# A two-layer block on one core: a joined gate, earlier statistics, lent tiles for the fifth scan, and a reordered end

## The chip, the core and the metric

The kernel runs on one core of one Trainium2 chip. The metric is the device time of one execution in microseconds (us), here always of that core. The engines are TensorE (PE in the profile, its weight loads PEld), VectorE (DVE), ScalarE (ACT), GpSimd (POOL) and SyncE (SP), which issues most DMAs. Each engine works through its own queue in the order in which the program wrote its instructions, and waits on semaphores for the others.

## The reference, cut to what matters

The input x has 4 batches of 256 tokens of width 512, in float32. Layer 0 adds an attention with small latents and a gated FFN of width 1792, both on the normalized x. Layer 1 adds a selective state-space model (below) and a top-2 mixture of LoRA experts over a dense product, again on the normalized x.

```python
proj = hidden_states @ in_proj_w            # 512 -> 2 * 1024
x, z = jnp.split(proj, 2, axis=-1)
xc = silu(conv4(x))                         # causal taps along time, per channel
ssm_p = jnp.einsum('bdl,ed->ble', xc, x_proj_w)
dt_r, Bm, Cm = rmsnorm of ssm_p[:32], [32:48], [48:64]
dt = softplus(dt_r @ dt_proj_w.T + dt_bias)
def step(h, inp):                           # over 256 time steps, 1024 channels x 16 states
    dA = jnp.exp(dt_t[..., None] * A)
    h = dA * h + dt_t[..., None] * B_t[:, None, :] * x_t[..., None]
    return h, jnp.einsum('bdn,bn->bd', h, C_t)
y = (ys + D_param[None, :, None] * xc) * silu(z)
out = jnp.einsum('bdl,hd->blh', y, out_proj_w)
```

## The kernel before, in words

The program is written out by hand in one function, and a schedule by hand fixes the order of each engine's queue. Layer 0 takes up the first 285 us: layer norm, attention of batches 0 to 3, and beside it the FFN as a generator `ff` whose pieces `go(ff, n)` puts between the attention's steps. `gate_up` makes the hidden values, `down` multiplies them by the down projection and adds the result to x. For token blocks 5, 6 and 7 the sum is kept in PSUM, and `add_last` adds it later, within layer 1.

Layer 1 works on one batch after another. The scan of a batch is cut into 32 units: 8 chunks c of 128 channels, times 4 groups g of 4 states each. `NU` is 4, `PER` is 32, and the loop at L1370 has one pass u for each of the 128 units, and two more. A unit consists of:

- `decays(u)`, ACT: four exponentials of dt times A into a tile of 128 x 1024 (L978). The loop issues it two units ahead.
- `scan_in(u)`, DVE: bx, the product of the B row and the spread dt*x (L984).
- `scan(u)`, DVE: the scan itself into a tile h (L999), and on POOL the product hc of h and the C row (L1004).
- `states_sum(u)`, PE: adds hc over the states into ysum in PSUM (L1016). For the first group of a chunk it begins ysum with D times xc (L1014). It is issued in pass u + 1.

When the four groups of a chunk are summed, `take_sum` copies ysum out (L1021, on ACT; on DVE for the very first), two units after the last group's scan. One unit later `gate` multiplies it by silu(z) on POOL (L1024). `ysum` has one buffer, so the next chunk's sum begins after `take_sum`.

Between these, `put(b, s, f, ...)` places other work at unit s of batch b, ahead of that unit's bx; `put_mid` places it between bx and scan, `put_late` behind the scan. In batch b this other work is: the rest of dt for the same batch (`step_in` on PE and ACT into tile `u`, `step_exp` on ACT into `u`, `lw` and `e`, `step_out` and `step_x` on POOL); dt and dt*x sent to DRAM and read back with each channel spread over the partitions of its states (`send`, L931, and `spread`, L937, both on SP); z's projection (`pz_mm`, L946) and its silu (`gate_silu`, L952, with a table load before and after it); and for the next batch b + 1 the norm (`norm_stats`, `norm_scale`, `norm_turn`, `norm_copy`), x's projection (`px_mm`, L755), the convolution (`conv_in`, `conv_taps`, `conv_out`; some taps as matmuls, L802, some on POOL, L809), its silu (`conv_silu`, L818), the product with x_proj (`pp_mm`, L829) and its rms norm (`pp_square`, `pp_norm`, L843). Batch 0 also loads the late weights (`load_late`, L1232: rl for the router, lb, bw, ow), and batches 0 and 2 hold the `router` and the choice of experts (`route`). The output of batch b - 1 is multiplied in batch b (`out_mm`, L1112). For the last batch it follows in a list `late` at the end of the loop, from unit 118 on; then `out_x` copies each half to x (L1117) and issues its store (L1118).

A tile of a pool with a tag shares the buffers of that tag: a new tile waits until all who use the old one in that buffer are done, also where they stand later in the program. Four cases matter here. The PSUM tag `mm` has 3 buffers. The weight tag `w_in` has 3, and `weights` issues its load on SP (L621), so a load whose buffer is not free holds SP's whole queue. The tags `u`, `e` and `lw` have one each. The pool `act`, with tiles h (2), hc (3), sz (3) and two of the three decay tiles, is opened at the end of pass 2 in the memory of the FFN's hidden values (`open_act`), and so can be written only after the last down projection. This is why the first scans take their tiles from others: `lent` names, for units 0 to 3, the tags in which decays, h and hc lie.

Of the kernel before, what the change touches and what calls it, by code (L numbers as in the profile page):

```python
# [8 lines left out]
F32 = mybir.dt.float32  # L9
# [3 lines left out]
ALU = mybir.AluOpType  # L13
# [28 lines left out]
def block_kernel(  # L42
# [508 lines left out]
    ff = gate_up(0)  # L551
    masks()

    def maxima(b, pieces, second, side=()):

        side = dict(side)
        for k in range(8):
            for hp in range(2):
                scores_max(b, k, hp)
            for f, *args in side.get(k, ()):  # L560
                f(*args)
            go(ff, pieces[k])
            if k in (3, 5, 7):
                put_max(b, k // 2 - 1)
            go(second, 1)
        go(second)
# [41 lines left out]
    ff = gate_up(1)  # L608
    attention(2, ff, True, 6)
    norm = normalize(2)  # L610
    attention(3, ff, False, 5, {k: [(next, norm)] for k in range(6)})
    go(ff, 1)
    weigh(3, 7)
    att.close()
# [97 lines left out]


    def norm_stats(b):
        mv = w1.tile([P, 2, 2], F32, tag="mv1", name="mv1", bufs=2)
        for i in range(2):
            st = w1.tile([P, 6], F32, tag="st1", name="st1", bufs=2)
            nc.vector.bn_stats(st, x[:, 2 * b + i, :])
            nc.vector.bn_aggr(mv[:, i, :], st)
        rs = w1.tile([P, 2], F32, tag="rsn", name="rsn", bufs=2)  # L720
        inv_root(rs, mv[:, :, 1], eps[:, 0:1])
        live["ln", b] = mv, rs
# [226 lines left out]
    def gate_silu(b, *ps):  # L949
# [5 lines left out]


    lent = {
        "d": ("d", "w_in", "d", "w_in"), "h": ("w_in", "u", "e", "u"),
        "hc": ("w_in", "lw", "w_in", "lw"),
    }  # L960

    def lend(n, u):
# [149 lines left out]
        mm(live["po", b, i], lhsT=xcs[b][:, c, i * P : (i + 1) * P], rhs=late_w["ow"][:, c, :],  # L1112
           start=False, stop=(c == DC - 1))

    def out_x(b, i):
        tb = 2 * b + i
        nc.scalar.copy(x[:, tb, :], live.pop(("po", b, i)))  # L1117
        nc.sync.dma_start(out_d[tb * P : (tb + 1) * P, :], x[:, tb, :])  # L1118


    def load_x(b, p):
# [128 lines left out]
    for b in range(B):  # L1250
# [14 lines left out]
        else:  # L1265
# [5 lines left out]
            put_late(b, 2, step_x, b, 1)  # L1271
            put(b, 4, load_z, b, 1)
            put(b, 9, load_late, "rl")
            put(b, 11, load_late, "lb")
            for k in range(4):
                put(b, 14 + 2 * k, load_late, "bw", k, 4)
            for k in range(DC):
                put(b, 21 + k, load_late, "ow", k, DC)
            for p, u in ((0, 3), (1, 8)):
                for i in range(2):  # L1280
                    put(b, u, pz_mm, b, p, i)
            put(b, 4, gate_silu, b, 0)
            put(b, 12, gate_silu, b, 1)
            put_late(b, 1, add_last, 5)
            put_late(b, 3, add_last, 6)
            put_late(b, 4, add_last, 7)
# [14 lines left out]
            put(b, 3 if c == 2 and not b else 4 * c - 6 + o, spread, "dt", b, c)  # L1301
            put(b, 4 * c - 4 + o, spread, "du", b, c)
        put(b, 10, load_z, b, 2)
        put(b, 12, load_z, b, 3)
        for p, at_i, at_g in ((2, (14, 15), 16), (3, (22, 24), 25)):
            for i in range(2):
                put(b, at_i[i], pz_mm, b, p, i)
            if p == 3 or nxt == B:
                put(b, at_g, gate_silu, b, p)
        if nxt < B:  # L1310
# [11 lines left out]
                put(b, 8 + o + 2 * p, conv_in, nxt, p)  # L1322
                put(b, 9 + o + 2 * p, conv_taps, nxt, p)
            put(b, 16 + o, conv_out, nxt, NP - 1)
            put(b, 16 + o, conv_silu, nxt, (b, 2))
            put(b, 17 + o, pp_mm, nxt, 0)
            put(b, 18, pp_mm, nxt, 1)
            put(b, 19, pp_square, nxt)
# [19 lines left out]
            for k, u in enumerate((27, 28, 29, 31)):  # L1348
                put(b, u, pz_mm, nxt, k // 2, k % 2)
            if b % 2 == 0:  # L1350
                for i, u in enumerate((16, 19, 20, 21)):
                    put(b, u, router, b, i)
                put(b, 25, route, b)
            put(b, 26, expert_turn, b)
# [11 lines left out]
            put(b, 21, expert_out, b, 1)  # L1366

    total = B * PER
    late = []
    for u in range(total + 2):  # L1370

        last = u - 2
        shut = (last // PER, last % PER // NU) if last >= 0 and last % NU == NU - 1 else None
        if shut and shut != (0, 0) and u < total:
            take_sum(*shut)
        if 3 <= u < total - 2:
            decays(u + 2)
        for f, a in at.get(u, ()):
            f(*a)
        if u < total:  # L1380
            if u:
                scan_in(u)
            for f, a in mid_at.get(u, ()):
                f(*a)
        if shut == (0, 0):
            take_sum(0, 0)
        if u > total:
            b, c = shut
            nc.vector.tensor_tensor(xcs[b][:, c, :], ysum, szs[b, c // 2][:, c % 2, :], ALU.mult)
        if u < total:  # L1390
            scan(u, 1 if u < total - 1 else 4)
            if u < 3:
                decays(u + 2)
        if u < total and u > NU + 1 and u % NU == 2:
            gates = (u - NU - 2) // NU
            gate(gates // DC, gates % DC)
        for f, a in late_at.get(u, ()):
            f(*a)
        if late and u >= total - PER + 22:
            c = late.pop(0)  # L1400
            for i in range(2):
                out_mm(B - 1, i, c)
        if total > u > total - PER and u % NU == 2 and (u - NU - 2) // NU >= total // NU - DC:
            late.append((u - NU - 2) // NU % DC)
        if u > total:
            late.append(DC - 1)
        if 1 <= u <= total:
            states_sum(u - 1)
        if u < 3:
            go(ff, (9, 12, 100)[u])  # L1410
        if u == 2:
            open_act()
    for i in range(2):
        for c in late:
            out_mm(B - 1, i, c)
        out_x(B - 1, i)


# [99 lines left out]
```

## Time and profile before

| what | us |
|---|---|
| median of 4 runs (lowest to highest) | 842.02 (839.02 to 843.23) |
| the profiled execution, its own time | 841.21 |
| its span, first to last instruction | 839.4 |
| start of scan 0, of scan 32 (batch 1), of scan 127 | 326.19, 467.34, 825.39 |
| last matmul of the down projection ends | 346.9 |
| last copy of the output ends | 836.1 |
| busy: PE, DVE, ACT, POOL | 749.6, 654.1, 552.8, 497.0 |
| granted TensorE clock, mean | 0.953 |

A line of a timeline gives the start, the duration of a group of like instructions in a row, the engine, the line of the kernel, the operation, the tile written and the tiles read, the shape, and the count. A bracket gives the idle time of that engine before it and who ended the wait. Matmuls in float32 appear as two records each, so "x8" is four matmuls. Lines of the page's second part hold one digit per fortieth of the span (21 us): the busy share in tenths.

### The profile page before, as it was taken

The numbers are of one execution on the slowest core, as the hardware profiler recorded it, in microseconds if no ns is written. First come the engines' busy times: TensorE is split into PE (matmuls) and PEld (weight loads), VectorE is DVE, ScalarE is ACT, GpSimd is POOL, SyncE is SP. The second block draws the span as 40 slices with busy tenths as digits, with TensorE's granted clock in tenths as the row PEclk, the third lists the DMA queues.
The fourth block names the chain that finished last, engine by engine and source line by source line (L and its number), as shares of the span: only waits on it lengthen the run. The fifth ranks groups of instructions, "written<-read, shape, count | busy, mean of one in ns | idle before, by whom it ended". The sixth has DMA issues, their size and how long they took to land.

```text
span 839.4 us, 11100 instructions
## 1 busy us (share of the span) xinstructions
PE 749.6 (89%) x3846; PEld 430.4 (51%) x3846; DVE 654.1 (78%) x602; ACT 552.8 (66%) x1113; POOL 497.0 (59%) x389
## 2 busy tenths in 40 slices
PE   5999999999999999999787899997999987957874
PEld 3665546566555667666443457444357544313321
DVE  4587755387734446796899999999999999999994
ACT  4335575335556377689796898886998886856460
POOL 3233321002333424687869799779799679798763
PEclk9999999999999999979899999989999989997997
DMA  7234322002233322457663554444552435253200
GB/s 225 76 89 127 100 76 63 0 1 55 70 86 82 108 39 79 135 139 186 146 158 102 150 154 125 111 113 126 157 158 88 113 94 143 65 155 109 83 18 25
DMA packets 68642, 86.71 MB, mean 103 GB/s; under 512 B 12221, under 2 KB 52169, under 8 KB 68458
## 3 DMA queue, kind: packets, MB, share of 16 engines
q1 hardware_dynamic: 58938, 66.08, 29.2%
q0 software_dynamic: 9072, 18.35, 7.8%
q10 hardware_dynamic: 576, 1.57, 0.5%
q8 instruction: 30, 0.49, 0.2%
q14 instruction: 26, 0.21, 0.1%
HBM read 66.58 MB, written 10.22 MB: 91 GB/s over the span
## 4 chain that ended last, share of the span: by engine, by line
PE 47%; DVE 28%; ACT 12%; POOL 7%; issue 4%; DMA 2%; SPq 0%; DVEq 0%; ACTq 0%; POOLq 0%
DVE h L999 17%; PE pg L444 6%; ACT decay L978 6%; PE pu L444 5%; PE po L469 5%; DVE bx L984 5%; POOL hc L1004 5%; PE px L755 4%; PE av L397 4%; PE ysum L1016 2%; PE scT L386 2%; PE px L802 2%; DVE mpl L354 2%; PE po L1112 2%; PE po L464 2%
## 5 line engine op out<-in xcount | busy, mean ns | idle before, releaser
L1004 POOL TENSOR_TENSOR hc<-h,cr 128x1024 f32<-128x1024 f32 (+1 forms) x130 | 301.9, 2324 | 75.7 <-DVE h L999 59.7
L999 DVE TENSOR_TENSOR_SCAN h<-decay,bx 128x1024 f32<-128x1024 f32 (+1 forms) x129 | 288.2, 2236 | 26.1 <-POOL hc L1004 4.9
L978 ACT ACTIVATE decay<-dts,aneg 128x255 f32<-128x255 f32 x504 | 213.3, 501 | 52.7 <-DVE h L999 42.6
L984 DVE TENSOR_TENSOR bx<-brow,dus 128x1024 f32<-128x1024 f32 x128 | 157.7, 1232 | 7.1 <-DMA dus<-dud 2.8
L1016 PE MATMUL ysum<-hc,stack 128*32 128x256 f32 x1024 | 87.3, 417 | 39.6 <-POOL hc L1004 39.5
L456 POOL TENSOR_TENSOR hlo<-g,hhi 128x512 fp32r<-128x512 f32 x28 | 35.8, 1280 | 117.3 <-ACT hhi L455 117.3
L354 DVE TENSOR_REDUCE mpl<-sc 128x4 f32<-128x1024 f32 x64 | 76.7, 1219 | 23.6 <-PE sc L352 22.1
L427 POOL DMA_DIRECT2D wgu<-in_wgu x56 | 31.0, 555 | 90.8 <-PE pg L444 89.6
L1112 PE MATMUL po<-ow,xc 128*128 128x512 f32 x128 | 70.9, 659 | 12.0 <-POOL xc L1024 11.4
L388 ACT ACTIVATE pe<-scT 128x1024 f32<-128x1024 f32 x64 | 64.0, 1023 | 22.9 <-PE sc L352 14.3
L1016 PEld LDWEIGHTS ysum<-hc,stack 128*32 128x32 f32 x1024 | 21.1, 111 | 99.1 <-POOL hc L1004 63.2
L946 PE MATMUL pz<-xn1T,w_in 128*128 128x256 f32 x256 | 71.4, 429 | 0.0
L755 PE MATMUL px<-xn1T,w_in 128*128 128x256 f32 x256 | 62.7, 392 | 0.4 <-ACT sz L952 0.3
L946 PEld LDWEIGHTS pz<-xn1T,w_in 128*128 128x128 f32 x256 | 51.8, 212 | 20.9 <-issue 13.4
L755 PEld LDWEIGHTS px<-xn1T,w_in 128*128 128x128 f32 x256 | 48.7, 194 | 13.8 <-issue 3.4
L452 DVE SCALAR_TENSOR_TENSOR g<-g,pg 128x512 f32<-128x512 f32 x28 | 19.2, 686 | 45.5 <-ACT g L451 45.5
L469 PE MATMUL po<-wd,hhi 128*128 128x512 f32 x112 | 49.2, 439 | 0.0
L444 PE MATMUL pg<-xhi,wgu 128*128 128x512 f32 x112 | 48.8, 435 | 0.0
L444 PE MATMUL pu<-xhi,wgu 128*128 128x512 f32 x112 | 47.7, 426 | 0.8 <-DVE g L454 0.8
L455 ACT CAST hhi<-g 128x512 fp32r<-128x512 f32 x28 | 17.3, 619 | 45.8 <-DVE g L454 45.8
L444 PE MATMUL pu<-xlo,wgu 128*128 128x512 f32 x112 | 44.5, 397 | 0.0
L444 PE MATMUL pg<-xlo,wgu 128*128 128x512 f32 x112 | 44.1, 394 | 0.0
(236 smaller groups left out, 1271.4 us busy)
## 6 DMA issues: line engine op xcount, KB each, us to landing
dts<-dtd SPq DMA_DIRECT2D x124, 128.0 KB, 2.8
dus<-dud SPq DMA_DIRECT2D x124, 128.0 KB, 3.1
wgu<-in_wgu POOLq DMA_DIRECT2D x56, 256.0 KB, 2.7
w_in<-in_inz SPq DMA_DIRECT2D x16, 512.0 KB, 4.7
w_in<-in_inx SPq DMA_DIRECT2D x14, 512.0 KB, 4.3
dtd<-dt SPq DMA_DIRECT2D x15, 256.0 KB, 2.2
dud<-du SPq DMA_DIRECT2D x15, 256.0 KB, 2.2
wd<-in_wd POOLq DMA_DIRECT2D x7, 512.0 KB, 3.5
```

What stands on the lines that cost most here:

```text
L354: nc.vector.tensor_reduce(mpl2[b % 2][:, qb, 2 * hp : 2 * hp + 2, 16 + 2 * gq : 18 + 2 * gq], sc.rearrange("p i (f k) -> p i f k", f=2), A ...
L388: nc.scalar.activation(pes[b, k][:, 2 * t : 2 * t + 2, :], sc, AF.Exp)
L444: mm(ps, lhsT=wgus[i][:, hc, :], rhs=xs[j][:, hc, :], start=(hc == 0 and j == 0), stop=(hc == HC - 1 and j == 1))
L469: mm(po, lhsT=hids[th][j][:, m, i * P : (i + 1) * P], rhs=wd[:, m, :], start=False, stop=(m == MC - 1 and j == 1))
L755: mm(px[:, i, :], lhsT=w[:, i, hc, :], rhs=xns[b][:, hc, :], start=(hc == 0), stop=(hc == HC - 1))
L946: mm(pz[:, i, :], lhsT=w[:, i, hc, :], rhs=xns[b][:, hc, :], start=(hc == 0), stop=(hc == HC - 1))
L978: nc.scalar.activation(da[:, k, 1:], live["dts", b, c][:, k, 1:], AF.Exp, scale=aneg[:, c, k, g : g + 1])
L984: nc.vector.tensor_tensor(bx, brow[g // 2][:, g % 2, :].unsqueeze(1).to_broadcast([P, NG, S]), live["dus", b, c], ALU.mult)
L999: nc.vector.tensor_tensor_scan(h[:, n].rearrange("p n t -> p (n t)"), da[:, n].rearrange("p n t -> p (n t)"), bx[:, n].rearrange("p n t -> ...
L1004: (nc.vector if k == NG - 1 else nc.gpsimd).tensor_tensor(hc[:, n], h[:, n], crows[b][:, g, :].unsqueeze(1).to_broadcast([P, NG // parts, ...
L1016: mm(ysum[k * NB : (k + 1) * NB, :], lhsT=stack, rhs=hc[:, k, :], start=False, stop=(g == NU - 1))
L1112: mm(live["po", b, i], lhsT=xcs[b][:, c, i * P : (i + 1) * P], rhs=late_w["ow"][:, c, :], start=False, stop=(c == DC - 1))
```

## The change

- The statistics (bn_stats, bn_aggr) of batch 1's norm move from unit 2 of batch 0 into layer 0, at step 6 of the last attention; a function `moments` holds them, with one buffer per tag.
- The fifth scan (unit 4) takes h from tag `e` and hc from tag `u`, no longer from `act`.
- The copy of the very first sum, on DVE, stands behind the scan of unit 5, not ahead of it.
- In batch 0 the projection of z's pair 1 moves from unit 8 to units 11 and 12, its silu from unit 12 to the convolution's silu at unit 17, and the gate of chunk 2 to that of chunk 3 at unit 18. Pair 2's projection moves from units 14 and 15 to 15 and 16, the first `router` from 16 to 18.
- In batch 0 the load of z's pair 3 moves from unit 12 to 17, lb from 11 to 22, bw from 14, 16, 18, 20 to 18 to 21, ow from 21 to 28 to 22 to 29.
- In the last batch each gate stands one unit earlier, in the pass of its `take_sum`; the sum over states stands ahead of the output matmuls of the list `late`.
- The last gate, on DVE, is cut into two halves of 128 tokens. The second half of the output is copied by DVE and stored from ACT's queue.

```diff
@@ -550,6 +550,13 @@
     hidden(0)
     ff = gate_up(0)
     masks()
+
+    def moments(b, pool):
+        mv = live["mv"] = pool.tile([P, 2, 2], F32, tag="mv1", name="mv1")
+        for i in range(2):
+            st = pool.tile([P, 6], F32, tag="st1", name="st1")
+            nc.vector.bn_stats(st, x[:, 2 * b + i, :])
+            nc.vector.bn_aggr(mv[:, i, :], st)
 
     def maxima(b, pieces, second, side=()):
 
@@ -608,7 +615,7 @@
     ff = gate_up(1)
     attention(2, ff, True, 6)
     norm = normalize(2)
-    attention(3, ff, False, 5, {k: [(next, norm)] for k in range(6)})
+    attention(3, ff, False, 5, {**{k: [(next, norm)] for k in range(6)}, 6: [(moments, 1, pre)]})
     go(ff, 1)
     weigh(3, 7)
     att.close()
@@ -712,11 +719,9 @@
 
 
     def norm_stats(b):
-        mv = w1.tile([P, 2, 2], F32, tag="mv1", name="mv1", bufs=2)
-        for i in range(2):
-            st = w1.tile([P, 6], F32, tag="st1", name="st1", bufs=2)
-            nc.vector.bn_stats(st, x[:, 2 * b + i, :])
-            nc.vector.bn_aggr(mv[:, i, :], st)
+        if b > 1:
+            moments(b, w1)
+        mv = live["mv"]
         rs = w1.tile([P, 2], F32, tag="rsn", name="rsn", bufs=2)
         inv_root(rs, mv[:, :, 1], eps[:, 0:1])
         live["ln", b] = mv, rs
@@ -955,8 +960,8 @@
 
 
     lent = {
-        "d": ("d", "w_in", "d", "w_in"), "h": ("w_in", "u", "e", "u"),
-        "hc": ("w_in", "lw", "w_in", "lw"),
+        "d": ("d", "w_in", "d", "w_in"), "h": ("w_in", "u", "e", "u", "e"),
+        "hc": ("w_in", "lw", "w_in", "lw", "u"),
     }
 
     def lend(n, u):
@@ -1112,10 +1117,10 @@
         mm(live["po", b, i], lhsT=xcs[b][:, c, i * P : (i + 1) * P], rhs=late_w["ow"][:, c, :],
            start=False, stop=(c == DC - 1))
 
-    def out_x(b, i):
+    def out_x(b, i, side=0):
         tb = 2 * b + i
-        nc.scalar.copy(x[:, tb, :], live.pop(("po", b, i)))
-        nc.sync.dma_start(out_d[tb * P : (tb + 1) * P, :], x[:, tb, :])
+        (nc.vector.tensor_copy if side else nc.scalar.copy)(x[:, tb, :], live.pop(("po", b, i)))
+        (nc.scalar if side else nc.sync).dma_start(out_d[tb * P : (tb + 1) * P, :], x[:, tb, :])
 
 
     def load_x(b, p):
@@ -1271,16 +1276,15 @@
             put_late(b, 2, step_x, b, 1)
             put(b, 4, load_z, b, 1)
             put(b, 9, load_late, "rl")
-            put(b, 11, load_late, "lb")
             for k in range(4):
-                put(b, 14 + 2 * k, load_late, "bw", k, 4)
+                put(b, 18 + k, load_late, "bw", k, 4)
+            put(b, 22, load_late, "lb")
             for k in range(DC):
-                put(b, 21 + k, load_late, "ow", k, DC)
-            for p, u in ((0, 3), (1, 8)):
+                put(b, 22 + k, load_late, "ow", k, DC)
+            for p, us in ((0, (3, 3)), (1, (11, 12))):
                 for i in range(2):
-                    put(b, u, pz_mm, b, p, i)
+                    put(b, us[i], pz_mm, b, p, i)
             put(b, 4, gate_silu, b, 0)
-            put(b, 12, gate_silu, b, 1)
             put_late(b, 1, add_last, 5)
             put_late(b, 3, add_last, 6)
             put_late(b, 4, add_last, 7)
@@ -1301,8 +1305,8 @@
             put(b, 3 if c == 2 and not b else 4 * c - 6 + o, spread, "dt", b, c)
             put(b, 4 * c - 4 + o, spread, "du", b, c)
         put(b, 10, load_z, b, 2)
-        put(b, 12, load_z, b, 3)
-        for p, at_i, at_g in ((2, (14, 15), 16), (3, (22, 24), 25)):
+        put(b, 12 if b else 17, load_z, b, 3)
+        for p, at_i, at_g in ((2, (14, 15) if b else (15, 16), 16), (3, (22, 24), 25)):
             for i in range(2):
                 put(b, at_i[i], pz_mm, b, p, i)
             if p == 3 or nxt == B:
@@ -1322,7 +1326,7 @@
                 put(b, 8 + o + 2 * p, conv_in, nxt, p)
                 put(b, 9 + o + 2 * p, conv_taps, nxt, p)
             put(b, 16 + o, conv_out, nxt, NP - 1)
-            put(b, 16 + o, conv_silu, nxt, (b, 2))
+            put(b, 16 + o, conv_silu, nxt, (b, 2) if b else (b, 1, 2))
             put(b, 17 + o, pp_mm, nxt, 0)
             put(b, 18, pp_mm, nxt, 1)
             put(b, 19, pp_square, nxt)
@@ -1348,7 +1352,7 @@
             for k, u in enumerate((27, 28, 29, 31)):
                 put(b, u, pz_mm, nxt, k // 2, k % 2)
             if b % 2 == 0:
-                for i, u in enumerate((16, 19, 20, 21)):
+                for i, u in enumerate((16 if b else 18, 19, 20, 21)):
                     put(b, u, router, b, i)
                 put(b, 25, route, b)
             put(b, 26, expert_turn, b)
@@ -1366,7 +1370,7 @@
             put(b, 21, expert_out, b, 1)
 
     total = B * PER
-    late = []
+    late, gated = [], []
     for u in range(total + 2):
 
         last = u - 2
@@ -1382,38 +1386,44 @@
                 scan_in(u)
             for f, a in mid_at.get(u, ()):
                 f(*a)
-        if shut == (0, 0):
-            take_sum(0, 0)
         if u > total:
             b, c = shut
-            nc.vector.tensor_tensor(xcs[b][:, c, :], ysum, szs[b, c // 2][:, c % 2, :], ALU.mult)
+            for i in range(2):
+                w = slice(i * P, (i + 1) * P)
+                nc.vector.tensor_tensor(xcs[b][:, c, w], ysum[:, w], szs[b, c // 2][:, c % 2, w], ALU.mult)
         if u < total:
             scan(u, 1 if u < total - 1 else 4)
+            if shut == (0, 0):
+                take_sum(0, 0)
             if u < 3:
                 decays(u + 2)
-        if u < total and u > NU + 1 and u % NU == 2:
-            gates = (u - NU - 2) // NU
-            gate(gates // DC, gates % DC)
+
+        for g in range(2):
+            o = u - NU - 1 - g
+            if u < total and o >= 0 and o % NU == 0 and (o >= total - PER) == (g == 0):
+
+                for c in (2, 3) if o == 3 * NU else (o % PER // NU,) if o != 2 * NU else ():
+                    gate(o // PER, c)
+                if g == 0:
+                    gated.append(o % PER // NU)
         for f, a in late_at.get(u, ()):
             f(*a)
+        if 1 <= u <= total:
+            states_sum(u - 1)
         if late and u >= total - PER + 22:
             c = late.pop(0)
             for i in range(2):
                 out_mm(B - 1, i, c)
-        if total > u > total - PER and u % NU == 2 and (u - NU - 2) // NU >= total // NU - DC:
-            late.append((u - NU - 2) // NU % DC)
-        if u > total:
-            late.append(DC - 1)
-        if 1 <= u <= total:
-            states_sum(u - 1)
+        late, gated = late + gated, []
         if u < 3:
             go(ff, (9, 12, 100)[u])
         if u == 2:
             open_act()
+    late.append(DC - 1)
     for i in range(2):
         for c in late:
             out_mm(B - 1, i, c)
-        out_x(B - 1, i)
+        out_x(B - 1, i, i)
 
 
 # ---- launch: one core; the host lays the weights out as the program reads them ----
```

## The prediction

> **What bounds the kernel now.** All times are microseconds from the start of the profiled span. I call pass n of the loop at L1370 unit n: one multiplication bx (1.23, L984) and one scan (2.29, L999) on DVE, so 128 units, 32 for each batch. First I read the busy tenths of the page: DVE is at 9 almost everywhere from slice 24 on, but at 6 to 9 before, and PE at 9 up to slice 20.
>
> ```profile
> PE   5999999999999999999787899997999987957874
> DVE  4587755387734446796899999999999999999994
> ```
>
> Then I read the timeline of DVE in batch 0 (326 to 467), where the starts of two scans should lie 3.69 apart (1.23 + 2.29 and two gaps). It is the stage with stalls: scan 0 starts at 326.19, scan 32 at 467.34, 141.2 for what takes 32 x 3.69 = 118.1. From scan 32 to scan 127 there are 95 scans in 358.1, 3.77 each. So batch 0 and the end are where this change can matter. The brackets tell what ended a stall:
>
> ```profile
> 342.17 1.23 DVE L984 TENSOR_TENSOR bx<-brow,dus 128x1024 f32<-128x1024 f32 x1
> 346.99 2.29 DVE L999 TENSOR_TENSOR_SCAN h<-decay,bx 128x1024 f32<-128x1024 f32 x1 [3.59 <-PE po L469]
> ...
> 387.99 2.29 DVE L999 TENSOR_TENSOR_SCAN h<-decay,bx 128x1024 f32<-128x1024 f32 x1 [2.53 <-POOL hc L1004]
> ...
> 396.42 1.23 DVE L984 TENSOR_TENSOR bx<-brow,dus 128x1024 f32<-128x1024 f32 x1 [2.46 <-DMA dus<-dud]
> ...
> 419.72 0.48 DVE L843 SCALAR_TENSOR_TENSOR nrm<-pp,lnw,rs 64x256 f32<-64x256 f32 x1 [1.36 <-ACT rs L711]
> ```
>
> Four stalls with four releasers: scan 4 waits for the last down projection, scan 14 for a buffer that POOL frees, unit 16 for a spread DMA, unit 21 for the chain that makes batch 1's nrm. Third, the timeline of ACT, which shows who feeds them:
>
> ```profile
> 346.94 3.30 ACT L978 ACTIVATE decay<-dts,aneg 128x255 f32<-128x255 f32 x8 [7.28 <-PE po L469]
> ...
> 356.49 0.45 ACT L873 ACTIVATE u<-pdt,vec 128x256 f32<-128x256 f32 x1
> ...
> 371.75 0.37 ACT L1021 COPY xc<-ysum 128x256 f32<-128x256 f32 x1 [2.24 <-PE ysum L1016]
> ...
> 385.64 1.28 ACT L952 ACT_TABLE_LOAD   x1
> 386.93 0.60 ACT L952 ACTIVATE sz<-pz 128x512 f32<-128x512 f32 x1
> 387.54 1.28 ACT L706 ACT_TABLE_LOAD   x1
> ```
>
> ACT starts at 346.94, when PE ends the down projection, and has no gap until 369.5. Fourth, busy time by stretches (us, then busy of PE, weight load, DVE, ACT, POOL, the granted clock, DMA):
>
> ```profile
> 355.20:365.50 10.30, 10.12 (x42) 5.24 (x41) 9.80 (x7) 10.27 (x24) 6.94 (x5) 0.50 0.71 170
> 365.50:374.50 9.00, 9.00 (x54) 6.61 (x50) 8.54 (x6) 6.69 (x15) 8.81 (x5) 1.00 0.41 111
> 374.50:405.30 30.80, 29.90 (x174) 21.53 (x170) 23.06 (x14) 27.96 (x71) 25.45 (x20) 1.00 0.55 139
> ```
>
> PE is full from 355 to 405, at half clock for the first 10. So between 347 and 405 it is the chain PE-ACT, not DVE, that sets the pace, and what DVE gains before must wait for it.
>
> **The change part by part, units 0 to 10.** (1) Statistics: unit 2 loses two bn_stats and two bn_aggr, 332.71 to 334.33, 1.62 of DVE. They go to the third attention, beside DVE gaps of 2.7 to 3.5 (266.1 to 269.6, 272.6 to 275.3), so I cost them nothing there; without that cover 1.7. Scan 2 starts at 334.0. (2) Lent tiles: scan 4 no longer waits for the FFN's memory and starts near 342.0, not 346.99. But the next on DVE is add_last(7), which waits for the same projection, 346.95; then bx, and scan 5 at 348.85 instead of 351.76, which also needs a decay that ACT ends at 348.6. POOL gains nothing: its hc of unit 3 lies behind the memset of 346.96. (3) The first sum behind scan 5: 351.4 to 351.8, as now, since ysum is ready at 351.36. Scan 6 at 353.1 (355.44 before), scan 7 at 356.5 (359.13), where decay 7 ends. So DVE is 2.6 ahead at unit 7.
>
> The price is in what ACT does next. The Abs at 356.49 (step_in, unit 5) writes tile u, in which the fifth scan's hc now lies. It must wait for the sum of unit 4 on PE, which is queued behind the transposes and ends at 357.89. No row shows this wait; its bounds are 0 (PE earlier) and 1.45, and I take 1.45, since all that PE does before it hangs on ACT work that doesn't move. Behind the Abs stand three more, two copies, and decays 8 to 10: decay 8 ends at 362.0 instead of 360.55, decay 10 at 371.0 instead of 369.5. So scan 8 starts at 362.05 (362.81 before) and scan 10 at 371.05 (370.18): the lead is spent.
>
> (4) pz of pair 1 moves from unit 8 to units 11 and 12: PE loses 3.72 (365.66 to 369.38) there. But with 1.4 more of waiting for the Relu at 358, then for ACT's copy of the second sum (371.35) and for the first taps, PE starts the taps at 373.75 (374.55 before): 0.8 of the 3.72 remain. (5) From there to the sum of unit 15, PE takes 30.7 now (374.55 to 405.25), with 0.8 of gaps. It loses the router (1.1) and gains pz: 30.7 - 0.8 - 1.1 + 3.7 = 32.5, so 406.3 instead of 405.25. (6) The second gate joined to the third: ACT loses two table loads and a silu at unit 12, 3.2. This hid PE; with ACT free, PE is late next, so 0 of 3.2 arrive. At unit 17 the silu comes back, 0.58. Decay 20: 413.02 + 1.05 + 0.58 = 414.65, scan 20 at 416.4 (414.81 before). On POOL the gate of 0.73 moves from unit 14 to 18, where POOL has a gap of 3.25 after it: nothing. (7) The router of unit 16 now stands at unit 18 behind pp on PE, ahead of the sum and the square that nrm waits for: 1.1. pp starts 1.0 later, but its half clock ended at 416.66, so it ends 0.6 later: nrm and scan 21 come 0.6 + 1.1, about 1.8 late (421.9). From scan 21 on DVE has no wait above 0.5: 1.8 stays to unit 32.
>
> (8) Loads on SP: z of pair 3 (512 KB), lb and half of bw (256 KB each piece) leave a stretch (381 to 399) where DMA moved 3.95 MB at 200 to 270 GB/s. But z of pair 2 now waits for pz at unit 12, 386.0 instead of 380.03, and the dt and du writes and spreads of chunk 4 stand behind it on SP. Its du landed 16.4 after that point (396.4); with 1.28 of 3.95 MB gone, 11 after 386, at 397, against 396.4. Nothing, with a bound of +6.
>
> **The end.** In the last batch gates come a unit earlier, and the sums stand ahead of the output matmuls. Rows now, PE then POOL:
>
> ```profile
> 822.85 1.08 PE L1016 MATMUL ysum<-hc,stack 128*32 128x256 f32 x8 [3.03 <-POOL hc L1004]
> 827.22 3.78 PE L1112 MATMUL po<-ow,xc 128*128 128x512 f32 x4 [3.28 <-POOL xc L1024]
> 830.93 1.93 PE L1016 MATMUL ysum<-hc,stack 128*32 128x256 f32 x16
> 833.48 1.98 PE L1112 MATMUL po<-ow,xc 128*128 128x512 f32 x4 [0.62 <-DVE xc L1389]
> ```
>
> ```profile
> 826.44 0.72 POOL L1024 TENSOR_TENSOR xc<-xc,sz 128x256 f32<-128x256 f32 x1
> ```
>
> The last hc pieces are there at 829.4, but PE is in chunk 6's output matmuls until 831.0. After: that gate is done at 823.5; the matmuls follow the sum at 823.9 and end near 827.0 (half clock until about 826.3, as after 812.6, where one stretch of 3.4 sufficed). hc, without the gate before it, ends at 828.8, the sums at 829.1. The final gate in halves (0.42 whole, 0.2 to 0.4 each) lets the first half's matmuls start at 829.45; the second half's end at 831.4; its copy on DVE (0.64, from the copy of the same shape at L1205) ends at 832.2 instead of 836.08. The output's issue on ACT's queue costs 0.33 as the w_in issue at 279.1; I count no difference to SP. So 3.9 less; if the clock stays at half (matmuls 3.78 and 1.93 as now), 1.3 less.
>
> [...] The profile's half clock follows stretches in which PE was little busy (0.42 of 3.40 at 819.4, 1.43 at 351.8). [...]
>
> **Sum.** +1.8 - 3.9 = -2.1. The profiled execution took 841.21 (span 839.4), 0.8 below the median of 842.02; it would come to 839.1, and the median to **839.9**.
>
> **Rivals.** A: the Abs doesn't wait, and PE isn't halved before pp (6.30, of which 5.4 at half clock; 3.6 at full). Then the taps start 1.4 earlier, pp ends early enough, and scan 21 is paced by DVE, at 418.7: -1.4 - 3.9, 836.7, down to 834.5 if the half-clocked 10.3 after 355 shrinks too. For it: PE's gaps decide, and they shift. Against: the Abs is behind nothing that gets faster. B, slower: SP stands behind z of pair 2. If DMA stays as crowded as now, du of chunk 4 lands at 402.4, unit 16 starts 5.3 late, and the 1.28 MB moved behind unit 17 (5.8 at 220 GB/s) push the spreads of chunk 6 by up to 3.5: 1.8 + 5.3 + 3.5 - 3.9 = +6.7, with slack on DVE behind it about 847. It decides from a batch 0 that is 8.1 late. Against: DMA share is 0.55 over 374 to 405. C: the end does not do what it says, PE at half clock throughout: +1.8 - 1.3, 842.5.
>
> **Numbers.** Forecast 0.43, A 0.30, B 0.12, C 0.15. Half a percent (4.2), about what a measurement of this kernel can tell from no change, puts the bounds at 837.8 and 846.2: faster 0.30 (A), same 0.58 (forecast and C), slower 0.12. The range leaves out B and the lower edge of A: 834.5 to 845.
>
> **What would show it.** Right: scan 4 at about 342 and scan 10 no earlier than 370; an ACT wait of about 1.4 for ysum at 356.5; no table load near 386 but ACT waiting for PE there; scan 32 at 468 to 470; less than 4 between the last scan's end and the last copy's (8.3 now). Wrong: scan 10 at 368 (the lead survives), a DVE wait for dus at unit 16 above 4, or half clock at 829.

## The result and the profile after

The changed kernel takes 842.36 us (median of 51 runs, 836.37 to 846.29). The kernel before, run on the same chips, takes 838.65 (median of 77 runs, 836.03 to 843.41), not the 842.02 of the four runs shown. The ratio on record is **1.0038 [1.0027, 1.0048]**, so the change costs 0.0038 x 838.65 = 3.2 us (the quotient of the two medians alone would be 1.0044). The prediction had a gain of 2.1. Its time (839.9) was only 2.5 off, but the direction was wrong, and a part of the closeness is luck: the four runs it started from were late ones.

| | before | after |
|---|---|---|
| profiled execution, us | 841.21 | 841.86 |
| its span, us | 839.4 | 840.1 |
| last down projection ends | 346.90 | 346.31 |
| scan 21 starts | 420.12 | 423.01 |
| scan 32 starts | 467.34 | 470.54 |
| scan 64 starts | 588.14 | 592.23 |
| scan 127 starts | 825.39 | 829.52 |
| last scan's end to span's end | 11.62 | 8.15 |

All times are microseconds from the start of the span, units as in the prediction; in layer 1 the line numbers of after are 4 to 7 higher than those of before. First the busy tenths of the page of after:

```profile
PE   5999999999999999979798899988999986976985
DVE  4587754297735437876889999998999999999996
```

PE's row of nines ends at slice 17 (counted from 1), where before it ended at 19; slice 18 begins at 357, in batch 0. DVE reaches the steady 9 no sooner. In the table scan 32, the first of batch 1, is 3.2 late, and scan 127 is 4.1 late, so most of the loss is in batch 0. The timeline of DVE there:

```profile
341.96 2.29 DVE L1004 TENSOR_TENSOR_SCAN h<-decay,bx 128x1024 f32<-128x1024 f32 x1
...
361.75 2.29 DVE L1004 TENSOR_TENSOR_SCAN h<-decay,bx 128x1024 f32<-128x1024 f32 x1 [1.99 <-ACT decay L983]
...
370.69 2.29 DVE L1004 TENSOR_TENSOR_SCAN h<-decay,bx 128x1024 f32<-128x1024 f32 x1 [1.69 <-ACT decay L983]
...
397.60 1.23 DVE L989 TENSOR_TENSOR bx<-brow,dus 128x1024 f32<-128x1024 f32 x1 [3.71 <-DMA dus<-dud]
...
416.44 2.29 DVE L1004 TENSOR_TENSOR_SCAN h<-decay,bx 128x1024 f32<-128x1024 f32 x1 [2.86 <-ACT decay L983]
...
422.61 0.48 DVE L848 SCALAR_TENSOR_TENSOR nrm<-pp,lnw,rs 64x256 f32<-64x256 f32 x1 [2.62 <-ACT rs L718]
```

These are scans 4, 8, 10, the multiplication of unit 16, scan 20 and nrm. Scan 4 is 5 earlier than before, scan 10 0.5 later, nrm 2.9 later: the lead of the lent tiles is gone after six units, as expected, and then more is lost than the 1.8 that was expected. It is behind nrm's releaser, ACT. The timeline of ACT in after:

```profile
357.54 0.47 ACT L878 ACTIVATE u<-pdt,vec 128x256 f32<-128x256 f32 x1 [1.56 <-PE ysum L1021]
...
387.21 0.47 ACT L819 ACTIVATE xc<-px,vec 128x256 f32<-128x256 f32 x1 [2.86 <-PE px L807]
...
418.79 0.27 ACT L1042 COPY ml<-pr 128x136 f32<-128x136 f32 x1 [2.44 <-PE pr L1040]
418.96 1.70 ACT L983 ACTIVATE decay<-dts,aneg 128x255 f32<-128x255 f32 x4
420.57 0.36 ACT L840 ACTIVATE sq<-pp 64x256 f32<-64x256 f32 x1
```

The first row is the Abs that now waits for tile u. The second is where the two table loads stood: ACT idles there and waits for PE. The last three are what the prediction missed. The square of pp, on which nrm hangs, stands in ACT's order behind a copy of the router's result (ml) and behind a decay. PE in after:

```profile
370.91 0.70 PE L1019 MATMUL ysum<-xc,dgs 128*128 128x256 f32 x2 [1.48 <-ACT xc L1026]
...
373.29 2.00 PE L807 MATMUL px<-pad,dg 128*128 128x256 f32 x8 [1.11 <-ACT dg L777]
...
405.75 0.64 PE L1021 MATMUL ysum<-hc,stack 128*32 128x256 f32 x8
...
412.43 5.20 PE L834 MATMUL pp<-xc,xpw 128*64 128x256 f32 x16 [4.28 <-ACT xc L823]
417.56 1.19 PE L1040 MATMUL pr<-rl,xn1T 128*128 128x136 f32 x8
```

The same place in before, PE and then ACT:

```profile
411.29 6.30 PE L829 MATMUL pp<-xc,xpw 128*64 128x256 f32 x16 [4.27 <-ACT xc L818]
```

```profile
413.02 3.30 ACT L978 ACTIVATE decay<-dts,aneg 128x255 f32<-128x255 f32 x8
417.63 0.38 ACT L835 ACTIVATE sq<-pp 64x256 f32<-64x256 f32 x1 [1.31 <-PE pp L829]
```

In before pp ends at 417.59 and its square starts at once. In after pp ends at 417.63 (412.43 + 5.20), and its square starts 2.9 later, at 420.57. That pp ends no later is the clock's doing: it starts 1.1 later, but only 3.1 of it ran at half clock, and 5.4 in before. The first two rows of PE in after show the gaps that pz of pair 1 filled before (1.48 + 1.11).

The end, PE and then DVE in after:

```profile
827.99 3.78 PE L1117 MATMUL po<-ow,xc 128*128 128x512 f32 x4
831.70 1.93 PE L1021 MATMUL ysum<-hc,stack 128*32 128x256 f32 x16
834.01 1.98 PE L1117 MATMUL po<-ow,xc 128*128 128x512 f32 x4 [0.38 <-DVE xc L1393]
```

```profile
833.67 0.49 DVE L1393 TENSOR_TENSOR xc<-ysum,sz 128x128 f32<-128x128 f32 x2 [0.71 <-PE ysum L1021]
836.03 0.69 DVE L1122 COPY x<-po 128x512 f32<-128x512 f32 x1 [1.88 <-PE po L1117]
```

The last scan starts at 829.52 and ends at 831.94, the last copy ends at 836.72: 4.78, where it was 8.27 (827.81 to 836.08). The last output matmuls start 0.34 after the halved gate does, whose two halves take 0.49: they no longer wait for the whole of it.

### The profile page after: what moved, and what is told of

The parts are those of the page before. It is cut to its first block, busy times and chain, and to the rows that moved or that the text cites. A ratio compares the mean times of both kernels' runs of the same rounds, so it can differ in the third digit from the quotient of the medians.

```text
span 840.1 us, 11102 instructions
## 1 busy us (share of the span) xinstructions
PE 750.3 (89%) x3846; PEld 429.1 (51%) x3846; DVE 656.3 (78%) x604; ACT 549.8 (65%) x1110; POOL 496.7 (59%) x389
## 4 chain that ended last, share of the span: by engine, by line
PE 51%; DVE 24%; ACT 13%; POOL 6%; issue 4%; DMA 1%; DVEq 0%; SPq 0%; ACTq 0%; POOLq 0%
DVE h L1004 14%; ACT decay L983 7%; PE pg L444 6%; PE pu L444 5%; PE po L469 5%; POOL hc L1009 4%; PE av L397 4%; PE px L760 4%; DVE bx L989 3%; PE px L807 3%; PE ysum L1021 3%; PE pz L951 3%; PE po L1117 2%; PE scT L386 2%; DVE mpl L354 2%
## 5 line engine op out<-in xcount | busy, mean ns | idle before, releaser
L1021 PE MATMUL ysum<-hc,stack 128*32 128x256 f32 x1024 | 89.3, 422 | 38.4 <-POOL hc L1009 38.4
L354 DVE TENSOR_REDUCE mpl<-sc 128x4 f32<-128x1024 f32 x64 | 76.7, 1219 | 23.6 <-PE sc L352 22.2
L1117 PE MATMUL po<-ow,xc 128*128 128x512 f32 x128 | 73.0, 676 | 4.5 <-POOL xc L1029 4.1
L951 PE MATMUL pz<-xn1T,w_in 128*128 128x256 f32 x256 | 68.8, 416 | 0.0
L951 PEld LDWEIGHTS pz<-xn1T,w_in 128*128 128x128 f32 x256 | 49.8, 204 | 20.4 <-issue 13.6
```

What stands on the lines that cost most here:

```text
L354: nc.vector.tensor_reduce(mpl2[b % 2][:, qb, 2 * hp : 2 * hp + 2, 16 + 2 * gq : 18 + 2 * gq], sc.rearrange("p i (f k) -> p i f k", f=2), A ...
L951: mm(pz[:, i, :], lhsT=w[:, i, hc, :], rhs=xns[b][:, hc, :], start=(hc == 0), stop=(hc == HC - 1))
L1021: mm(ysum[k * NB : (k + 1) * NB, :], lhsT=stack, rhs=hc[:, k, :], start=False, stop=(g == NU - 1))
```

## The experiments

Twelve kernels were run; each ratio is to the kernel before on the same chip, with its 95% interval. A scan's time in this part, "scan 21" above all, is its start counted from the end of the last down projection, so that what happened earlier drops out: 73.2 before, 76.7 after.

### First: the change in three parts, each put on the kernel before

**The end alone** (earlier gates in the last batch, sums ahead of the matmuls, halved gate, second copy on DVE).

```diff
-        if u < total and u > NU + 1 and u % NU == 2:
+        for g in range(2):
+            o = u - NU - 1 - g
+            if u < total and o >= 0 and o % NU == 0 and (o >= total - PER) == (g == 0):
...
-        out_x(B - 1, i)
+        out_x(B - 1, i, i)
```

> The kernel before with only the end of the change: gates of the last batch one unit earlier, sums ahead of the output matmuls, the last gate in halves, the second copy on DVE and its store from ACT's queue. My theory (the end gains, batch 0 loses): scans as before to the last one, then 11.6 from the last scan's end to the end of the span become about 8.2, so 3.4 less, ratio 0.996. Rival (the end gains nothing that a median shows, since the clock of PE falls there by chance): ratio 1.000.

Measured: 0.9973 [0.9952, 0.9994], 835.86. The last scan's end lies 8.13 ahead of the span's end, 3.5 less than before, as in after. All traces with this end have 8.1 there, all without it 11.0 to 11.6. The end does what it says; in after it does so with PE at half clock (0.50 from 827.99 to 831.70).

Its trace showed something else. Up to the last batch this kernel is the same program as before, yet scan 21 starts at 69.8, 3.4 sooner. Busy time by stretches (start:end, us, then busy of PE, weight load, DVE, ACT, POOL with their counts, the granted clock, DMA share, GB/s) of the kernel before, and then of this one:

```profile
351.80:355.20 3.40, 1.43 (x8) 0.77 (x7) 3.37 (x3) 3.37 (x5) 1.08 (x1) 1.00 0.37 143
355.20:358.60 3.40, 3.22 (x15) 1.65 (x15) 3.23 (x3) 3.40 (x10) 2.08 (x2) 0.50 0.24 80
358.60:365.40 6.80, 6.80 (x28) 3.59 (x26) 6.46 (x5) 6.77 (x15) 4.76 (x4) 0.50 0.94 216
```

```profile
349.10:352.50 3.40, 1.74 (x20) 0.79 (x8) 2.95 (x3) 3.36 (x4) 1.06 (x1) 1.00 0.53 169
352.50:355.90 3.40, 3.14 (x14) 2.30 (x18) 3.26 (x2) 3.40 (x9) 2.37 (x1) 0.50 0.00 0
355.90:366.20 10.30, 10.13 (x64) 7.05 (x60) 9.80 (x7) 10.20 (x20) 7.96 (x5) 1.00 0.77 191
```

In both, the clock is halved (0.50) behind a stretch of 3.4 in which PE was busy for 1.43 and for 1.74: for 10.2 in the trace of before, for 3.4 here. The trace from which the prediction was worked out was a late one; it took 2.6 more than the median of its kernel (841.21 - 838.65).

**The front alone** (statistics in layer 0, fifth scan in e and u, first sum behind scan 5).

```diff
-        "hc": ("w_in", "lw", "w_in", "lw"),
+        "hc": ("w_in", "lw", "w_in", "lw", "u"),
...
-        if shut == (0, 0):
-            take_sum(0, 0)
...
             scan(u, 1 if u < total - 1 else 4)
+            if shut == (0, 0):
+                take_sum(0, 0)
```

> The kernel before with only the front: statistics in layer 0, the fifth scan in tiles e and u, the first sum behind the sixth scan. My theory (ACT's Abs waits 1.5 for the sum of unit 4, and PE and ACT carry that to unit 21): scan 4 at about 342, an ACT wait of 1.5 ahead of the Abs of unit 5, scan 10 at 370 to 371, scan 21 by 0.5 to 1.5 later than before against the end of the down projection: ratio 1.001. Rival (the lead of DVE survives): scan 21 and the end 2.5 earlier, ratio 0.997.

Measured: 1.0039 [1.0016, 1.0061], 842.27. Scan 21 at 73.0, PE at half clock twice for 3.4, and the Abs waits 1.56 as in after. By itself this part costs. Where, its trace doesn't show: scan 21 is no later than before, and this execution (840.97) was 1.3 below the median of its kernel.

**The joined gate alone** (pz of pair 1 at units 11 and 12, pair 2 at 15 and 16, no gate at unit 12, router at 18, loads moved).

```diff
-            for p, u in ((0, 3), (1, 8)):
+            for p, us in ((0, (3, 3)), (1, (11, 12))):
...
-            put(b, 12, gate_silu, b, 1)
...
-                for i, u in enumerate((16, 19, 20, 21)):
+                for i, u in enumerate((16 if b else 18, 19, 20, 21)):
```

> The kernel before with only the joined gate and what goes with it: pair 1 of z's projection at units 11 and 12, its silu at 17, gates 2 and 3 together, the first router at 18, the loads later. My theory (PE sets the pace of units 5 to 17, the silu comes back at 17, and the router behind pp holds ACT's copy, and so the square that nrm waits for): scan 21 by 1.5 to 3 later than before, ratio 1.002 to 1.0035. Rival (two table loads saved are 2.6 saved): ratio 0.997. Rival (the spread of chunk 4 behind z of pair 2 on SP): scan 16 late by over 2 and all later scans with it.

Measured: 1.0096 [1.0066, 1.0127], 845.86, the dearest part (six runs), and far above the 1.0035 that was expected. Scan 21 at 76.8, 3.6 later than before, where after has 76.7. PE in this kernel, where pz was taken out:

```profile
369.68 0.70 PE L1014 MATMUL ysum<-xc,dgs 128*128 128x256 f32 x2 [2.96 <-ACT xc L1021]
...
372.06 3.63 PE L802 MATMUL px<-pad,dg 128*128 128x256 f32 x8 [1.11 <-ACT dg L772]
```

The gaps are 2.96 and 1.11, and the eight records of the taps take 3.63 instead of 2.00, so the clock is halved once more. The three parts do not add up: -0.27% + 0.39% + 0.96% is 1.1%, and the whole costs 0.4%.

**The front with hc of the fifth scan in lw, not u**, so that the Abs has nothing to wait for.

```diff
-        "hc": ("w_in", "lw", "w_in", "lw"),
+        "hc": ("w_in", "lw", "w_in", "lw", "lw"),
```

> As the front alone, but the fifth scan's product lies in tile lw, which ACT writes only at unit 7, so the Abs of unit 5 has no sum to wait for. My theory: the ACT wait ahead of that Abs is gone, decays 8 to 10 as before, scan 21 as before or up to 0.5 earlier, ratio 0.999 to 1.000, 1 to 1.5 less than the front with tile u. Rival (the wait is harmless, since PE is late anyway): the same time as the front with tile u.

Measured: 1.0008 [0.9982, 1.0034], 839.35. The Abs doesn't wait, and scan 10 is at 22.75 instead of 24.4 in after: locally the wait costs the 1.6 that it lasts. Yet scan 21 is at 73.4, no earlier than with u; here PE was at half clock for 10.2. The interval overlaps that of the front with u, so this pair alone doesn't settle the price.

### Second: one thing mended in the whole change

**The first router one unit later, behind the square.**

```diff
-                for i, u in enumerate((16 if b else 18, 19, 20, 21)):
+                for i, u in enumerate((16 if b else 19, 19, 20, 21)):
```

> The changed kernel, but the first router of batch 0 stands at unit 19, behind the square of pp, not at 18. My theory (at 18 ACT's copy of the router's result waits for PE, and decay 21 and the square that nrm waits for stand behind it): the square on ACT starts about 2.5 earlier against pp's end, nrm and scan 21 come 2.5 earlier, ratio to before 1.0005 to 1.001 instead of 1.0038. Rival (the loss is in the units before 17): the same time as the changed kernel.

Measured: 1.0007 [0.9991, 1.0023], 839.09. ACT in this kernel, at the same place as above:

```profile
413.66 3.29 ACT L983 ACTIVATE decay<-dts,aneg 128x255 f32<-128x255 f32 x8
417.71 0.38 ACT L840 ACTIVATE sq<-pp 64x256 f32<-64x256 f32 x1 [0.75 <-PE pp L834]
```

Both decays now run ahead of the square, which starts as soon as pp is there. The square starts 2.9 sooner against pp's end. Scan 21 is at 75.05, 1.7 sooner than in after and not the 2.5 expected, since pp itself ended 1.2 later here, with PE at half clock for 13.7 after 351.8. One number in one line is worth 0.0031 x 838.65 = 2.6, and its interval doesn't overlap that of the whole change. The router's place is a cause.

**pz of pair 1 back at unit 8**, the rest of the change as it is.

```diff
-            for p, us in ((0, (3, 3)), (1, (11, 12))):
+            for p, us in ((0, (3, 3)), (1, (8, 8))):
```

> The changed kernel, but pair 1 of z's projection is back at unit 8 (its silu and gate stay at 17 and 18). My theory (moved away it left PE idle for 3 us before the second sum's copy, and it then filled PE where PE sets the pace): PE has no gap over 1.5 between units 8 and 10, the sum of unit 15 ends 2 to 3 earlier against the end of the down projection, ratio to before about 1.001. Rival (ACT's wait for tile u makes PE late, so the gap is there anyway): at most 0.5 earlier, ratio 1.0035.

Measured: 1.0001 [0.9979, 1.0022], 839.10. PE in this kernel:

```profile
367.97 3.72 PE L951 MATMUL pz<-xn1T,w_in 128*128 128x256 f32 x16
...
376.85 2.00 PE L807 MATMUL px<-pad,dg 128*128 128x256 f32 x8
```

Between pz and the taps PE has no gap at all. The sum of unit 15 ends 58.1 after the projection, 60.1 in after. Scan 21 is only 0.6 sooner (76.1): in this execution (842.67, 3.6 above its median) the router still stood ahead of the square, and pp took 6.51 instead of 5.20. By all runs this mend is worth 0.0037 x 838.65 = 3.1, again with intervals that don't overlap. So pz's place is a cause too.

**hc of the fifth scan in lw, in the whole change.**

```diff
-        "hc": ("w_in", "lw", "w_in", "lw", "u"),
+        "hc": ("w_in", "lw", "w_in", "lw", "lw"),
```

> The changed kernel, but the fifth scan's product lies in tile lw, so the Abs of unit 5 doesn't wait. The front alone cost 1.0039 with u and 1.0008 with lw, the joined part alone 1.0096, all together only 1.0038, so the costs don't add. My theory now: with pair 1 moved away, PE idles ahead of the second sum in either case, and ACT sets the start of the taps: 1 to 1.5 earlier to unit 10, then PE-bound: ratio 1.002 to 1.003. Rival (the wait's whole cost comes off): 1.0007.

Measured: 1.0036 [1.0016, 1.0056], 841.89. Scan 10 comes 1.6 sooner here too, and the time stays. (Scan 21 is even later in its trace, 78.6, but that execution, 846.58, was 4.7 above its median, with PE at half clock for 6.8 from 374.2.) In the whole change the wait for u costs nothing that can be told.

**The load of z's pair 2 at unit 13**, so that SP doesn't stand ahead of du of chunk 4; this is the remedy for rival B.

```diff
-        put(b, 10, load_z, b, 2)
+        put(b, 10 if b else 13, load_z, b, 2)
```

> The changed kernel, but the load of z's pair 2 stands at unit 13 of batch 0, not 10, so SP doesn't hold the writes and spreads of chunk 4 behind it. My theory (the DVE wait for dus at unit 16 is off the path, since PE and ACT pace units 17 to 21): the wait of 3.7 falls to under 1.5, scan 21 and the ratio stay: 1.003 to 1.004. Rival (SP's queue is a cause of the loss): scan 21 earlier by 1 to 3, ratio 1.000 to 1.0025.

Measured: 1.0031 [1.0014, 1.0048], 841.77. DVE at unit 16 in this kernel:

```profile
399.27 2.29 DVE L1004 TENSOR_TENSOR_SCAN h<-decay,bx 128x1024 f32<-128x1024 f32 x1 [3.64 <-POOL hc L1009]
```

The wait of 3.71 for dus is gone, and a wait of 3.64 for POOL has taken its place: scan 16 starts 52.48 after the projection, 52.65 in after. The DMA was merely the last to come; rival B is not the cause.

### Third: the parts put together without the two costs

The first two diffs are against the changed kernel, the third shows only what it adds to the second, and the last is against the kernel before. In the first, the lines that take the front out are not shown; in the last, those of the end.

**End, joined gate with pz at unit 8, router at 19; without the front.**

```diff
-            for p, us in ((0, (3, 3)), (1, (11, 12))):
+            for p, us in ((0, (3, 3)), (1, (8, 8))):
...
-                for i, u in enumerate((16 if b else 18, 19, 20, 21)):
+                for i, u in enumerate((16 if b else 19, 19, 20, 21)):
```

> The kernel before with the end of the change and the joined gate, but with pair 1 of z's projection left at unit 8 and the first router at unit 19; no lent tiles, no moved statistics. My theory (PE sets the pace of units 5 to 17, ACT the rest; this takes nothing from PE's early gap, takes the first router out of PE's full stretch and saves ACT two table loads): scan 21 by 2 to 4 earlier than with the end alone, ratio to before 0.992 to 0.995, below the 0.9973 of the end alone. Rival (the joined gate costs in itself, its silu on the path at unit 17): 0.998 to 1.001.

Measured: 0.9948 [0.9925, 0.9971], 833.58, as expected by the ratio. Scan 21 is at 71.5, not earlier than with the end alone (69.8) but later; here PE was at half clock for 10.2 after 352.0, there for 3.4.

**The whole change with both mends**, front with u.

```diff
-            for p, us in ((0, (3, 3)), (1, (11, 12))):
+            for p, us in ((0, (3, 3)), (1, (8, 8))):
...
-                for i, u in enumerate((16 if b else 18, 19, 20, 21)):
+                for i, u in enumerate((16 if b else 19, 19, 20, 21)):
```

> The changed kernel with both mended: pair 1 of z at unit 8, the first router at unit 19. Tile u still holds the fifth scan's product. My theory (the Abs waits 1.5 and here PE has no other gap to hide it): ratio 0.997 to 0.999, slower than the same without the front (0.9948). Rival (the two single gains of 3.1 and 2.7 add up, and the front is free): 0.994 to 0.995.

Measured: 0.9955 [0.9927, 0.9982], 835.40, scan 21 at 69.7 as with the end alone (69.8). My theory that the wait for u would still cost here fell: with the two mends the front costs nothing that can be told (0.9955 against 0.9948). The two mends together are worth 0.0083 x 838.65 = 7.0, a little more than 2.6 + 3.1.

**The same with hc in lw.**

```diff
-        "hc": ("w_in", "lw", "w_in", "lw", "u"),
+        "hc": ("w_in", "lw", "w_in", "lw", "lw"),
```

> As the one before, with the fifth scan's product in tile lw. My theory: the wait is gone, and the front's lead is still spent at unit 10 by ACT: ratio 0.994 to 0.996, the same as without the front (0.9948). Rival (the front's lead of 2 to 4 reaches the end once PE isn't late): 0.990 to 0.992.

Measured: 0.9977 [0.9956, 0.9999], 837.74, above what was expected, with an interval that overlaps the one with u. Scan 21 is at 71.3, with 10.2 of half clock. Taking the wait away buys nothing that can be seen here.

**End, and the router at 19; no joined gate and no front.**

```diff
-                for i, u in enumerate((16, 19, 20, 21)):
+                for i, u in enumerate((16 if b else 19, 19, 20, 21)):
```

> The kernel before with the end of the change and the first router at unit 19, nothing joined and nothing lent. My theory (ACT waits 2.3 for the router at unit 16, and PE does it in its full stretch): scan 21 by about 1 earlier than with the end alone, ratio 0.995 to 0.9965; what the joined gate adds to that is the rest to 0.9948. Rival (the whole gain of the best version over the end alone is the router's): 0.9948 or less.

Measured: 0.9945 [0.9926, 0.9964], 834.31, the rival's number; scan 21 at 69.4, 0.4 sooner than with the end alone. This and the one with the mended joined gate (0.9948) are the best versions, and they can't be told apart: **the joined gate, put right, adds nothing that these runs can tell.** The two intervals leave room for about 2.5 either way. Beside the end alone (0.9973) the later router may give 0.0028 more; the intervals overlap, so of the best gain only the end's share is shown.

## Why the prediction was wrong, step by step

**Right: steps 1 to 3, the start.** Scan 4 came at 341.96 (342.0 predicted), scan 5 at 348.30 (348.85), scan 8 at 361.75 (362.05), scan 10 at 370.69 (371.05), the Abs waited 1.56 (1.45). The lead was spent where the prediction said it would be. What the wait of the Abs costs in the end stayed small: by the whole change with u and with lw, 1.0038 against 1.0036, nothing that can be told. In the front alone the two differ by 0.3% with overlapping intervals, so its price there is open.

**Right: step 6, the table loads.** "0 of 3.2 arrive" holds: ACT waits 2.86 for PE where they stood, scan 20 is at 416.44 (416.4), and the end with the mended joined gate is no better than the end without it (0.9948 and 0.9945, both with the later router).

**Right: step 8, SP.** It was costed at nothing, with a bound of 6. The wait for du of chunk 4 grew from 2.46 to 3.71, and taking it away gained nothing that can be told from the whole change (1.0031 against 1.0038).

**Failed: step 7, the router at unit 18.** The prediction priced it as "1.1" on PE, ahead of the sum and the square. It moved the matmuls past pp and forgot the copy of their result, which moved too. That copy stands in ACT's queue ahead of decay 21 and the square. While PE multiplies (1.19), ACT waits, 2.44 in all, for the copy; then it does the decay (1.61 to the next start), and only then the square. So the matmuls and the decay don't run beside each other, and the square starts 2.9 after pp's end, where before it started at once: 2.9 in place of 1.1. By luck pp itself ended no later than before, 0.6 better than predicted, so nrm came only 1.1 later than predicted (422.61, predicted 421.5). The mend shows 2.6 by the ratios.

**Probably mis-sized: steps 4 and 5, pz of pair 1.** The prediction had the sum of unit 15 at 406.3, and it ended at 406.39, but that is partly luck: in after the down projection ended 0.6 sooner, and PE was at half clock for 3.4 twice, not for 10.2. Against that slow trace the taps were to start 0.8 sooner, and the move to cost 2.1 at this sum, about 1 net of the router's 1.1. The taps start 27.0 after the projection in after, 27.7 in before, but 25.3 with the end alone, where the half clock took 3.4. The mend measures 3.1 by the ratios, where the two intervals allow about 1 to 5, and 1.9 at this sum in the traces, with 10.2 of half clock in the mended one. So the price is shown to be there, its size only roughly. The two gaps of 1.48 and 1.11 stand where PE had pz to do before, and the same 3.72 then come in the stretch to unit 15, which has little room. One more half-clocked stretch there would have cost more: after had none at 372, the joined gate alone had one (3.63 instead of 2.00 for the taps).

**Right, a little smaller than predicted: the end.** 3.9 predicted, 3.5 in the trace (4.78 from the last scan's end to the last copy's, where less than 4 was named as the sign), and 0.0027 x 838.65 = 2.3 [0.5, 4.0] by the ratio of the end alone. The clock stayed at half through chunk 6's matmuls (0.50 from 827.99 to 831.70; they took 3.78, the sums 1.93, both as before), for which the prediction had 1.3 (rival C). It was wrong there: the order saves the time, since the sums need only wait for chunk 6's matmuls, which now run while the last scan does, and half a gate.

**The sum.** Against its own trace the prediction was 2.8 short (839.1, measured 841.86): 1.4 at scan 32 (469.1 and 470.54), 0.9 in batch 1, 0.4 at the end. The other 2.5 of the error of 5.3 is the base: the profiled execution of before is 2.6 above its median. That fits its trace beside the end alone, which is the same program there: 3.4 late at scan 21, most likely by the longer half clock, and 0.9 early from scan 32 to scan 64 (120.8, against 121.7 in after and 121.8 with the end alone). Batch 1 took 120.8 to 121.9 in all traces, with and without the change, so nothing says that its 0.9 is the change's. Scan 21 of after is 6.9 later than in the trace of the end alone, which was 1.8 below its median (834.02 and 835.86), while after's was 0.5 below its own: 5.6, and by the ratios the two kernels differ by 0.0065 x 838.65 = 5.5.

**The rivals.** A fell: the Abs waited. B had the sign, but not the mechanism, as the later load of z showed. C's clock came, C's price did not; that its 842.5 lies beside the measured 842.36 is chance, since it started from 842.02 and had 1.3 for the end. The case that happened, ACT held up for 2.44 by a moved copy, was none of them. A sign that the prediction named, scan 32 at 468 to 470, was just missed, with 470.54.

**Open.** What the wait for u costs in the front alone, and why the three parts cost 1.1% one by one and 0.4% together. The clock may be a part of it: among the five kernels with the new end, pz of pair 1 at unit 8 and no router at unit 18, scan 21 is at 69.4 to 69.8 in the three traces with 3.4 of half clock, and at 71.3 to 71.5 in the two with 10.2. But no run holds the clock fixed, so this is argued, not shown.

## What to carry to other kernels

When a matmul is moved, follow its result: the copy that takes it out of PSUM moves too, in the queue of another engine, and everything behind that copy in the queue waits for PE (here ACT for 2.44, and the square came 2.9 after pp); put the matmul where that engine has nothing urgent behind the copy. Work that keeps an engine busy ahead of its full stretch is not free to move into that stretch (pz of pair 1 cost 3.1 by the ratios), and a saving on the engine that waits for the full one arrives as nothing (0 of 3.2 on ACT). Before a change of half a percent is worked out from one trace, look at the spread of the runs: here one trace stood 2.6 from the median of its kernel, and the change was 3.2.

## What the runs showed of the hardware

- Two executions of the same instructions, before and the end alone up to the last batch, had PE at half clock for 10.2 and for 3.4 after a stretch of waiting at the same place. The half-clocked lengths seen between 351 and 381 in the traces are 3.4, 6.8, 10.2 and 13.7, so multiples of about 3.4.
- In before the clock was halved behind a stretch of 3.40 in which PE was busy for 1.43. It then stayed at half though PE was busy for 3.22 of 3.40 and for 6.80 of 6.80, and only then came back; with the end alone it was back after one stretch, with 3.14 of 3.40. Why it came back late in before isn't shown.
- The 77 times of the kernel before fall into bands: 18 from 836.03 to 837.14, 43 from 838.08 to 841.21, 16 from 842.51 to 843.41, and none in the gaps between. That the bands come from how long the clock stays halved is a guess from the two traces (10.2 and 3.4), and not shown.
